# A decoder layer on one core: the divisions of probabilities shared out anew over three engines, moments asked two steps sooner, scale diagonals at a step's head

## The chip, the core and the metric

The kernel runs on 1 core of one Trainium2 chip. The metric is device time in microseconds (us), taken as the median of the runs shown; smaller is better. The engines of the core are named as in the profile: PE (TensorE matmuls and transposes), PEld (its weight loads), DVE (VectorE), ACT (ScalarE), POOL (GpSimd) and SP (SyncE, which here only issues DMAs).

## The reference

One pre-norm decoder layer over 8 batches of 256 rows of 1024 numbers, all in float32, with a self-attention, an attention to a context and a feed-forward block. Cut to what matters:

```python
# x: (8, 256, 1024), ctx: (8, 256, 1024)
def bitnet_linear(x, weight, scale):          # weights become signs, a scale per output column
    s = max(mean(abs(weight), axis=1), 1e-8)
    y = x @ sign(weight / s[:, None]).T
    return nan_to_num(y * (s * scale), nan=0, posinf=1e6, neginf=-1e6)

def self_attention(h):                        # 32 heads of 32, 8 key/value heads, each for 4 heads
    q, k, v = bitnet_linear(h, qw, qs), bitnet_linear(h, kw, ks), bitnet_linear(h, vw, vs)
    p = softmax(q @ k.T / sqrt(32))
    return bitnet_linear(p @ v, ow, os)

def cross_attention(h, ctx):                  # 16 heads of 64, low rank
    c_q, c_kv = h @ Wq_d, ctx @ Wkv_d
    p = softmax((c_q @ W_qk) @ c_kv.T / 8)    # per head
    return p @ (c_kv @ Wv_u)

def ffn(h):                                   # rank 256, inner 2752
    g, u = split((h @ U1) @ V1 + b1)
    return ((silu(g) * u) @ U2) @ V2 + b2

x = x + self_attention(layernorm(x))
x = x + cross_attention(layernorm(x), ctx)
out = x + ffn(layernorm(x))
```

The softmax of the self-attention is what the change is about: `p = exp(s - max)`, and then each row of `p` is divided by its sum.

## The kernel before

The work runs in three phases: 8 batches of self-attention, each in 8 steps c0 to c7 of 4 heads (class `Self`); 8 batches of cross-attention, each in 4 steps of 4 heads (class `Cross`); then the feed-forward block in 4 blocks of 512 rows. Batches are written b0 to b7 below, so that "b3 c6" is step 6 of the fourth self-attention batch.

The order of the instructions is written out by hand (a manual schedule): every engine executes its instructions in the order in which the Python code emits them, and an instruction that waits holds up everything behind it on its own engine.

One call of `step(cur, prev, parts)` emits, in this order:

- 16 score matmuls of the step's own 4 heads (L547) into four PSUM score banks;
- `due.early()` and `due.late()` for the step before the last: ACT copies its weighted sum `po` to `oh` (L601), DVE forms the rest `ol` (L605);
- for each head, the row maximum `nm` (L689, DVE), and `turned`: four transposes of the PREVIOUS step's `p` (L524, PE), whose result ACT copies to `pT` (L528). So the divisions of one step are needed at the head of the next;
- `parts` pieces of projection work from a queue of `Part`s: the layernorm transposes of the next batch (`ln_parts`: `xn` L155, transposes L163, `xh` L344, `xl` L345), its q, k and v projections (matmuls L399 and L466, ACT scaling L408, then `nan_to_num`: L351, L354, L357 on DVE and L352, L353 on POOL), and the output projection of the batch before (`o_parts`: matmuls L492, `y` L501, `nan_to_num`, the residual sum L506 on POOL). In b0 there are also the turning of weights into signs (`weight`: transposes L163, ACT sign L309, sums L298 to L303) and the `scale_part`s, which spread a column of scales over all partitions: POOL builds diagonals `dg` (L327), PE multiplies them by ones (L334), DVE copies (L335);
- between the parts, the 8 exponentials of the step with their sums (L708, ACT), paced by the estimated time of the parts, and, as soon as the sums of two heads are there, `over_sums`: the reciprocal (L560, DVE) and the divisions of these heads on DVE (L570, two instructions per head) or POOL (L563, one per head); after all parts, `over_sums_end` puts the divisions meant for ACT (L577, two per head);
- last the 16 weighted-sum matmuls of the previous step (L584).

Who divides is `self.by`, a letter for each of the four heads: D for DVE, P for POOL, A for ACT. Before, it is AAPP in b0; elsewhere DPAA in c1 and c2, DDAA in c0 and c4, and DDDA in the other steps.

A `Part` can have an `ahead` piece (the `xn` of a layernorm part, the `dg` of a scale part), which is emitted before the part itself: for the first two parts at the step's head, for a later one when the part before it starts. A part marked `soon` (the layernorm parts) has its `ahead` emitted at the step's head wherever it stands in the step.

The moments of a layernorm row tile (two `bn_stats` L138 and one `bn_aggr` L140 for each of two tiles, and two small POOL instructions at the end) are not parts: they wait in the list `idle` and are emitted one by one by `run_part`, one for each 1.4 us of estimated part time. `ln_moments` puts those of the next batch but one at the list's front; `leave` puts those of a finished residual at its end. `need` flushes the list when a layernorm needs them.

All parts, the transposes and the projections take their PSUM bank from `bank()`, which turns through three banks; a bank is free again when the engine that copies it out (ACT or DVE) has done so.

Of the kernel before, what the change touches and what calls it, by code (L numbers as in the profile page):

```python
# [35 lines left out]
def decoder_layer(  # L36
# [25 lines left out]
    B, S, E = x.shape  # L62
    NT = B * S // P
    TB = S // P
    EC = E // P
# [41 lines left out]
    def bank(shape, name):  # L107
        turn[0] += 1
        if turn[0] % 3 == 1:
            return psB.tile(shape, F32, tag="psB", name=name)  # L110
        return psA.tile(shape, F32, tag="psA", name=name)
# [13 lines left out]
    idle, credit = [], [0.0]  # L125
# [46 lines left out]
    def settle():  # L172
        now = list(ripe)
        ripe[:] = later
        later.clear()
        for f in now:
            f()
# [3 lines left out]
    class Part:  # L181
        def __init__(self, us, main, ahead=None, soon=False):
            self.us, self.main, self.todo, self.soon = us, main, ahead, soon
# [5 lines left out]

    queue = []  # L190

    def run_part(then=None):

        settle()
        if then is not None:
            then()
        p = queue.pop(0)
        p.ahead()
        if queue:
            queue[0].ahead()  # L200
        p.main()
        credit[0] += p.us
        while idle and credit[0] > 1.4:
            credit[0] -= 1.4
            idle.pop(0)()
        if not idle:
            credit[0] = 0.0
# [7 lines left out]
    o_sc = wt.tile([P, E], F32, tag="o_sc", name="o_sc")  # L215
# [55 lines left out]
    for i in range(len(room), len(where)):  # L271
        last = max(k for k in range(i) if where[k] == where[i])
# [40 lines left out]
    def weight_next(i):  # L313

        weight_turn(i)
        weight_sum(i)
        for k in after.get(i, []):
            weight_load(k)

    def scale_part(col0, n, dst):  # L320

        box = {}

        def ahead():
            box["dg"] = wk_.tile([P, n, P], F32, tag="xn", name="dg", bufs=2)
            for k in range(n):
                nc.gpsimd.tensor_scalar_mul(  # L327
                    box["dg"][:, k, :], ident, scol[:, col0 + k : col0 + k + 1]
                )

        def main():
            ps = bank([P, n, P], "ps_d")
            for k in range(n):
                nc.tensor.matmul(ps[:, k, :], ones, box["dg"][:, k, :], start=True, stop=True)  # L334
            nc.vector.tensor_copy(dst, ps.rearrange("p k c -> p (k c)"))  # L335

        return Part(0.3 * n, main, ahead)

    def weight(i):
        return Part(1.1, lambda: weight_next(i))  # L340
# [97 lines left out]
    def q_parts(st, c0):  # L438
        return proj_T(
            st, lambda i, e: qT_w[c0 + i][:, e, :], c0, lambda: st.qT[:, c0 : c0 + 2, :]  # L440
        )
# [89 lines left out]
    class Self:  # L531


        def __init__(self, st, c):
            self.st, self.c = st, c

            self.by = (
                "AAPP" if st.b == 0 else "DPAA" if c in (1, 2) else "DDAA" if c % 4 == 0 else "DDDA"
            )

        def scores(self):
            st, c = self.st, self.c
# [29 lines left out]
        def over_sums_end(self):  # L572
            for j in range(4):
                if self.by[j] == "A":
                    for t in range(TB):
                        p = self.p[j][:, t, :]
                        nc.scalar.activation(p, p, AF.Copy, scale=self.sm[:, t, j : j + 1])  # L577

        def weighted(self, pTs):
            self.po = pso.tile([P, S], F32, tag="pso", name="po")  # L580
# [98 lines left out]
    def step(cur, prev, parts, extra=None):  # L679

        s = cur.scores()
        nm = small.tile([P, 4, TB], F32, tag="nm", name="nm")
        cur.sm = small.tile([P, TB, 4], F32, tag="sm", name="sm")
        due = prev.prev if prev is not None else None
        if due is not None:
            due.early()
        pTs = []
        for j in range(4):
            nc.vector.tensor_reduce(nm[:, j, :], s[j], AX.X, ALU.max, negate=True)  # L689
            if prev is not None:  # L690
                pTs.append(turned(prev.p[j]))
        for p in queue[: min(parts, 2)]:
            p.ahead()
        soon = [p for p in queue[:parts] if p.soon][:2]
        if isinstance(due, Cross):
            for p in soon:
                p.ahead()
        if due is not None:
            due.late()
        for p in soon:  # L700
            p.ahead()
        cur.p, cur.prev = [], prev
        exps = []

        def exp(j, t):
            if t == 0:
                cur.p.append(wk_.tile([P, TB, S], F32, tag="p", name="p", bufs=4))
            nc.scalar.activation(  # L708
                cur.p[j][:, t, :], s[j][:, t, :], AF.Exp,
                bias=nm[:, j, t : t + 1], accum_out=cur.sm[:, t, j : j + 1],  # L710
            )

        exps = [(j, t) for j in range(4) for t in range(TB)]


        divided = isinstance(cur, Self)
        pe, sc = 0.0, 0.5 if divided else 1.0
        pairs = [0, 1]
        for k in range(parts):
            pe += queue[0].us  # L720
            while exps and sc < pe:
                exp(*exps.pop(0))
                sc += 0.49

            def then():
                while k and divided and pairs and len(exps) <= 4 - 4 * pairs[0]:
                    cur.over_sums(pairs.pop(0))

            run_part(then)
            if k == 0 and extra is not None:  # L730
                extra()
        for e in exps:
            exp(*e)
        for i in pairs:
            cur.over_sums(i)
        cur.over_sums_end()
        if not parts and extra is not None:
            extra()
        if prev is not None:
            prev.weighted(pTs)  # L740
            prev.prev = None
        return cur
# [365 lines left out]
        nc.sync.dma_start(of[fb.i * BT + j], fb.x[j])  # L1108


    sts, xts = [], []
    for b in range(B):
        for l in (sts, xts):
            st = State()
            st.b = b
            l.append(st)

    def mixed(a, b):
        out = []
        for i in range(max(len(a), len(b))):  # L1120
            out += a[i : i + 1] + b[i : i + 1]
        return out
# [4 lines left out]
    def self_plan(b):  # L1127
        st = sts[b]
        if b == 0:
            nxt = sts[1]  # L1130
            v0 = v_parts(st)
            ln, k, v = ln_parts(nxt, 1), k_parts(nxt), v_parts(nxt)
            return [
                [weight(4), weight(5), v0[0], scale_part(10, 2, v_sc)]
                + [weight(6), v0[1], weight(7)],
                mixed(q_parts(st, 2) + q_parts(st, 4), [weight(8), weight(9), weight(10)]),
                mixed(q_parts(st, 6), [weight(11), weight(12)]),
                ln[:2] + [weight(13)] + ln[2:],
                mixed(k, [weight(14), weight(15)]),
                mixed(v, [weight(16), weight(17)]),  # L1140
                mixed(q_parts(nxt, 0), [weight(18), scale_part(12, 4, o_sc[:, 0:512])])
                + [weight(19)],
                mixed(q_parts(nxt, 2), [scale_part(16, 4, o_sc[:, 512:1024])]),
            ]
        o = o_all(sts[b - 1])
        if b + 1 < B:
            nxt = sts[b + 1]
            ln = ln_parts(nxt, b + 1)
            return [
                q_parts(st, 4) + q_parts(st, 6),  # L1150
                mixed(o[0], ln[:2]),
                mixed(o[1], ln[2:]),
                k_parts(nxt),
                o[2] + v_parts(nxt),
                o[3],
                q_parts(nxt, 0),
                q_parts(nxt, 2),
            ]
        x0 = xts[0]
        ln = lnx_parts(x0)  # L1160
        return [
            q_parts(st, 4) + q_parts(st, 6),
            o[0],
            o[1],
            mixed(o[2], ln[:2]),
            mixed(o[3], ln[2:]),
            ctx_parts(x0, (dve, act)) + ckv_part(x0),
            cq_part(x0) + ckvT_part(x0),
            cqk_parts(x0, (dve, act)),
        ]  # L1170
# [16 lines left out]
    def self_extra(b, c):  # L1187
        if b == 0 and c == 1:
            return lambda: ln_moments(sts[1], 1)
        if b + 2 < B and c == EC - 1:  # L1190
            return lambda: ln_moments(sts[b + 2], b + 2)

    def cross_extra(b, c):
# [39 lines left out]
    with tc.manual_schedule(  # L1233
# [8 lines left out]
        st = sts[0]  # L1242
# [41 lines left out]
        prev = None  # L1284
        for kind, sts_, plan, loads, extra, n in (
# [3 lines left out]
            for b in range(B):  # L1289
# [3 lines left out]
                for c in range(n):  # L1293
                    loads(b, c)
                    prev = step(kind(sts_[b], c), prev, len(ps_[c]), extra(b, c))


        pairs = [(fb, f) for fb in fbs for f in range(NF)]
# [76 lines left out]
```

## Time and profile before

| what | value |
|---|---|
| median of the runs | 1572.12 us (1571.53 to 1572.9) |
| profiled execution, its own time | 1571.7 us |
| its span from first to last instruction | 1569.9 us |
| mean granted PE clock | 0.992 |
| busy: PE, DVE, ACT, POOL | 96%, 62%, 52%, 25% of the span |
| self-attention phase, and in it b0 | 25.5 to 653.9 us; 25.5 to 133.8 us |
| one whole batch (b2) | 74.5 us |
| cross phase and feed-forward after it | 653.9 us to the end |

The profile is of one execution; its rows give the start in us from the span's beginning, the busy time, the engine, the line of the kernel and the tiles that an instruction writes and reads. "[0.81 <-ACT pT L528]" behind a row says that the engine was idle for 0.81 us ahead of it and that ACT's write of `pT` ended this wait. PEclk is the clock granted to PE as a share of full speed. A step's borders are taken at its first score matmul (L547).

### The profile page before, as it was taken

How to read it: one execution, taken by the hardware profiler on the slowest of the kernel's cores; microseconds unless marked ns; L12 is line 12 of the kernel's file. 1: busy time of each engine (PE TensorE's matmuls, PEld its weight loads, DVE VectorE, ACT ScalarE, POOL GpSimd, SP SyncE). 2: the span in 40 equal slices, each digit the busy share in tenths (PEclk: the TensorE clock that was granted, in tenths of full speed). 3: DMA queues.
4: the chain of work that ended last, by engine and by line, in shares of the span. 5: the costliest groups of instructions: out<-in, count | busy, mean ns of one | idle time of the engine just before them, and what ended most of it. 6: DMA issues, size and time to landing. Idle time of an engine off the chain costs nothing.

```text
span 1569.9 us, 25667 instructions
## 1 busy us (share of the span) xinstructions
PE 1513.1 (96%) x9494; PEld 1015.9 (65%) x9494; DVE 973.0 (62%) x1880; ACT 811.4 (52%) x2482; POOL 390.5 (25%) x474
## 2 busy tenths in 40 slices
PE   6889999999999999899999999999999999999998
PEld 5777787787878787677877777544444444444443
DVE  6777999999899989766676666333233223323322
ACT  3787888888888888745556666311111110111110
POOL 2435444444444434123221111100010002001102
PEclk9999999999999999999999999999999999999999
DMA  9420010101010132112254312120001002000001
GB/s 232 91 55 15 28 57 27 68 21 62 28 55 28 52 105 95 60 39 97 82 201 145 130 47 90 59 69 0 0 41 67 0 0 107 0 1 27 27 0 53
DMA packets 65611, 92.77 MB, mean 59 GB/s; under 512 B 40218, under 2 KB 46160, under 8 KB 65360
## 3 DMA queue, kind: packets, MB, share of 16 engines
q1 hardware_dynamic: 60880, 74.37, 15.3%
q0 software_dynamic: 4608, 16.78, 2.7%
q8 instruction: 75, 1.23, 0.3%
q14 instruction: 48, 0.39, 0.1%
HBM read 65.44 MB, written 25.17 MB: 58 GB/s over the span
## 4 chain that ended last, share of the span: by engine, by line
PE 77%; DVE 14%; ACT 6%; DMA 1%; issue 1%; POOL 0%; SPq 0%; POOLq 0%; DVEq 0%; ACTq 0%
PE ps_h L1034 19%; PE ps_z L1078 9%; PE ps_pt L524 8%; PE ps_o L492 5%; PE ps_q L399 5%; PE s L622 4%; PE po L645 4%; PE ps_p L1008 4%; DVE nm L689 4%; PE ps_o L1097 3%; ACT p L708 3%; PE s L547 2%; PE po L584 2%; PE ps_o L662 2%; PE ps_qk L863 2%; DVE p L570 2%
## 5 line engine op out<-in xcount | busy, mean ns | idle before, releaser
L708 ACT ACTIVATE p<-s,nm 128x256 f32<-128x256 f32 x768 | 357.7, 516 | 2.2 <-DVE nm L689 2.2
L528 ACT COPY pT<-ps_pt 128x512 f32<-128x512 f32 x384 | 198.4, 598 | 147.9 <-PE ps_pt L524 147.2
L1046 ACT ACTIVATE sg<-ps_h,b_col 128x512 f32<-128x512 f32 (+1 forms) x88 | 59.6, 678 | 413.5 <-PE ps_h L1034 413.5
L689 DVE TENSOR_REDUCE nm<-s 128x2 f32<-128x512 f32 x384 | 237.4, 679 | 10.0 <-PE s L622 6.8
L1047 DVE SCALAR_TENSOR_TENSOR sg<-ps_h,b_col,sg 128x512 f32<-128x512 f32 (+1 forms) x88 | 65.0, 739 | 274.4 <-ACT sg L1046 274.4
L524 PE MATMUL ps_pt<-ident,p 128*128 128x128 f32 x1536 | 196.4, 278 | 10.2 <-ACT pT L528 6.6
L524 PEld LDWEIGHTS ps_pt<-ident,p 128*128 128x128 f32 x1536 | 164.4, 141 | 51.8 <-issue 21.9
L708 ACT ACTIVATION_READ_ACCUMULATOR p<-s,nm 128x1 f32 x768 | 189.8, 247 | 0.0
L1107 POOL TENSOR_TENSOR x2t<-x2t,y 128x512 f32<-128x512 f32 x32 | 40.5, 1267 | 482.5 <-DVE y L1105 482.5
L1078 PE MATMUL ps_z<-ac,u_sb 128*128 128x512 f32 x336 | 157.7, 593 | 0.0
L399 PE MATMUL ps_q<-xh,qT_w 128*128 128x256 f32 x496 | 121.9, 287 | 1.1 <-ACT qT_w L309 1.1
L399 PE MATMUL ps_q<-xl,qT_w 128*128 128x256 f32 x496 | 118.9, 281 | 0.0
L352 POOL TENSOR_SCALAR tmp<-y 128x512 f32<-128x512 f32 x78 | 60.8, 780 | 216.5 <-DVE y L501 127.4
L1078 PEld LDWEIGHTS ps_z<-ac,u_sb 128*128 128x128 f32 x336 | 61.9, 190 | 68.8 <-issue 68.8
L492 PE MATMUL ps_o<-oT_w,oh 128*128 128x512 f32 x256 | 105.8, 413 | 0.0
L570 DVE TENSOR_SCALAR p<-p,sm 128x256 f32<-128x256 f32 x252 | 99.0, 448 | 9.6 <-DVE sm L560 1.4
L677 POOL TENSOR_TENSOR x1t<-x1t,y 128x256 f32<-128x256 f32 x64 | 47.6, 764 | 224.7 <-DVE y L670 224.7
L492 PE MATMUL ps_o<-oT_w,ol 128*128 128x512 f32 x256 | 100.9, 394 | 0.0
L577 ACT ACTIVATE p<-p,sm 128x256 f32<-128x256 f32 x200 | 87.8, 512 | 17.8 <-DVE sm L560 17.6
L399 PEld LDWEIGHTS ps_q<-xh,qT_w 128*128 128x128 f32 x496 | 93.3, 188 | 2.8 <-ACT qT_w L309 1.4
L399 PEld LDWEIGHTS ps_q<-xl,qT_w 128*128 128x128 f32 x496 | 93.4, 188 | 0.0
L1034 PE MATMUL ps_h<-pT,w_ffn 128*128 128x512 f32 (+1 forms) x184 | 88.7, 577 | 0.0
(159 smaller groups left out, 2736.4 us busy)
## 6 DMA issues: line engine op xcount, KB each, us to landing
xs<-in_x_dram SPq DMA_DIRECT2D x32, 512.0 KB, 4.1
x<-xs POOLq DMA_DIRECT2D x16, 512.0 KB, 3.0
x1t<-x SPq DMA_DIRECT2D x16, 512.0 KB, 6.0
c<-in_ctx_dram SPq DMA_DIRECT2D x16, 512.0 KB, 3.9
x<-x1t POOLq DMA_DIRECT2D x16, 512.0 KB, 3.8
x2t<-x SPq DMA_DIRECT2D x16, 512.0 KB, 5.8
out_dram<-x2t SPq DMA_DIRECT2D x16, 512.0 KB, 2.6
w<-in_L_attn_q_weight_dram SPq DMA_DIRECT2D x32, 128.0 KB, 5.7
```

Of the source, the lines that this page charges most:

```text
L399: nc.tensor.matmul(ps[:, i, :], w(i, e), x_[:, e, :], start=(e == 0 and x_ is st.xh), stop=(e == EC - 1 and x_ is st.xl),)
L492: nc.tensor.matmul(ps, o_[c // 4][:, c % 4, t * P : (t + 1) * P], oT_w[:, c, h * 512 : (h + 1) * 512], start=(c == 0 and o_ is st.oh), sto ...
L524: nc.tensor.transpose(ps[:, k, t * P : (t + 1) * P], p[:, t, k * P : (k + 1) * P], ident)
L528: nc.scalar.copy(pT, ps)
L570: nc.vector.tensor_scalar_mul(p, p, self.sm[:, t, j : j + 1])
L577: nc.scalar.activation(p, p, AF.Copy, scale=self.sm[:, t, j : j + 1])
L622: nc.tensor.matmul(s[2 * i + j][:, t, :], st.cqk[p0 : p0 + XD, 2 * c + i, t * P : (t + 1) * P], st.ckv[p0 : p0 + XD, :], start=True, stop= ...
L689: nc.vector.tensor_reduce(nm[:, j, :], s[j], AX.X, ALU.max, negate=True)
L708: nc.scalar.activation(cur.p[j][:, t, :], s[j][:, t, :], AF.Exp, bias=nm[:, j, t : t + 1], accum_out=cur.sm[:, t, j : j + 1],)
L1034: nc.tensor.matmul(ps[h * n : h * n + n], v1_of(r, i, f, n), fb.pT[:, r, h * w_ : (h + 1) * w_], start=(r == 0), stop=(r == RC - 1),)
L1047: nc.vector.scalar_tensor_tensor(sg[:m], hs[0][:m], bg, sg[:m], ALU.add, ALU.mult)
L1078: nc.tensor.matmul(fb.zs[r], fw.u2[f // 4][:n, f % 4, r * P : (r + 1) * P], ac[:n], start=(k == 0), stop=(k == NF - 1 and COPIES < 2),)
```

## The change

1. `self.by` is now read from a table `BY` of a string per step. In b0: DDDD, PPPD, PPPD, PPPP, PPPD, PPPD, DDDD, PPPD. In b1 to b6 only c1 and c2 change, from DPAA to PPAA. In b7, c1 and c2 become DDDA, c3 and c4 PPAA. In all, ACT loses 34 divisions (L577), POOL gains 17 (L563, one for a whole head), and DVE has as many as before: 26 more in b0, 24 fewer in b1 to b6, 2 fewer in b7.
2. The moments of the next batch but one are asked at c5 instead of c7.
3. The two scale parts of `o_sc` (b0 c6 and c7) are marked `soon`, so that their `dg` diagonals are built at the step's head.
4. `over_sums_end` is called before a part of over 1.0 us as soon as both pairs of heads are done, and not again later (the letters are blanked). It moves instructions only in c0 of b1 to b7, where ACT's four divisions now stand ahead of the last q scaling (L408).
5. In the last part of a step, `run_part` emits no moments (`last`).
6. In the very first step the exponentials are paced 2.5 us later (`sc` 3.0).

The orders of PE and of SP are the same in both kernels; those of DVE, ACT and POOL change.

```diff
-    def run_part(then=None):
+    def run_part(then=None, last=False):
...
-        while idle and credit[0] > 1.4:
+        while not last and idle and credit[0] > 1.4:
             credit[0] -= 1.4
             idle.pop(0)()
...
-    def scale_part(col0, n, dst):
+    def scale_part(col0, n, dst, soon=False):
...
-        return Part(0.3 * n, main, ahead)
+        return Part(0.3 * n, main, ahead, soon)
...
-            self.by = (
-                "AAPP" if st.b == 0 else "DPAA" if c in (1, 2) else "DDAA" if c % 4 == 0 else "DDDA"
-            )
+            self.by = st.by[c]
...
+            self.by = "    "          # at the end of over_sums_end
...
-        pe, sc = 0.0, 0.5 if divided else 1.0
+        pe, sc = 0.0, (0.5 if prev is not None else 3.0) if divided else 1.0
...
+            if divided and not pairs and queue[0].us > 1.0:
+                cur.over_sums_end()
...
-            run_part(then)
+            run_part(then, k == parts - 1)
...
+    BY = {
+        0: ["DDDD", "PPPD", "PPPD", "PPPP", "PPPD", "PPPD", "DDDD", "PPPD"],
+        1: ["DDAA", "PPAA", "PPAA", "DDDA", "DDAA", "DDDA", "DDDA", "DDDA"],
+        B - 1: ["DDAA", "DDDA", "DDDA", "PPAA", "PPAA", "DDDA", "DDDA", "DDDA"],
+    }
...
-                mixed(q_parts(nxt, 0), [weight(18), scale_part(12, 4, o_sc[:, 0:512])])
+                mixed(q_parts(nxt, 0), [weight(18), scale_part(12, 4, o_sc[:, 0:512], True)])
                 + [weight(19)],
-                mixed(q_parts(nxt, 2), [scale_part(16, 4, o_sc[:, 512:1024])]),
+                mixed(q_parts(nxt, 2), [scale_part(16, 4, o_sc[:, 512:1024], True)]),
...
-        if b + 2 < B and c == EC - 1:
+        if b + 2 < B and c == 5:
             return lambda: ln_moments(sts[b + 2], b + 2)
```

More of the change, by code (lines that the diff above doesn't have):

```diff
@@ L1115, in decoder_layer @@
             st.b = b
+            st.by = BY.get(b, BY[1])
             l.append(st)
```

## The prediction

> **What bounds the kernel now.** I read the page's busy line and chain first, then the list of what PE waits for, then windows of single steps.
>
> ```profile
> span 1569.9 us, 25667 instructions
> PE 1513.1 (96%) x9494; PEld 1015.9 (65%) x9494; DVE 973.0 (62%) x1880; ACT 811.4 (52%) x2482; POOL 390.5 (25%) x474
> PE 77%; DVE 14%; ACT 6%; DMA 1%; issue 1%; POOL 0%; SPq 0%; POOLq 0%; DVEq 0%; ACTq 0%
> ```
>
> PE is the bound, and the change leaves its instructions and their order alone. So only PE's lost time can be won, and new lost time is the only way to lose. I measured it per step: the step's length less its PE instructions at their undisturbed pitch (0.119 us for a 128x256 projection matmul, 0.232 for a 128x512 one, 0.109 for a transpose). An undisturbed step shows 0.60 by this measure. The steps above that: b0 c0 9.6, c1 3.0, c2 3.3, c3 6.9, c4 2.2, c5 1.6, c6 6.6 (c7 none); in b2 to b6 c1 1.60, c2 0.87, c3 1.75 (b1 only c3); b7 c4 2.1, c5 3.3, c7 2.95. In b1 to b6, c0 and c4 to c7 stand at the floor. The waits in PE's list that the change touches:
>
> ```profile
> PE ps_pt L524 <- ACT pT L528: 6.6, 8, 1.1
> PE ps_d L334 <- POOL dg L327: 6.4, 2, 4.0
> PE ps_t L163 <- DVE xn L155: 4.4, 6, 0.8
> ```
>
> (us in all, times, longest.) They sum to 17.4, most of what can be won.
>
> **The scale diagonals at the head of b0 c6.** Timeline:
>
> ```profile
> 116.58 2.22 POOL L563 TENSOR_TENSOR p<-p,sm 128x512 f32<-128x512 f32 x2 [0.49 <-DVE sm L560]
> 118.79 2.56 POOL L327 TENSOR_SCALAR dg<-ident,scol 128x128 f32<-128x128 f32 x4
> 119.63 2.57 PE L334 MATMUL ps_d<-dg,ones 128*128 128x128 f32 x8 [4.03 <-POOL dg L327]
> ```
>
> The four `dg` stand behind two divisions on POOL, and PE waits 4.03 us; its clock is at half from 117.51 to 124.34. With `soon` they stand at the step's head, where POOL is free, and the two POOL divisions of c6 are gone (DDDD). The wait goes (4.0), and so does most of the half clock (c6 loses 6.6, floor 0.6, other transposes 0.7). I take −4.9. No DMA is issued by the moved pieces, and SP's queue is untouched.
>
> What is late next is c7. In c6 DVE now does eight divisions (DDDD, 8 × 0.35 = 2.8 us) and the first moments, where it did neither; behind them in its queue are `nm` of c7 and L335, which come some 2.4 us late: the exponentials and one transpose group waits 1.35, and the second `ps_d`, whose `dg` needs the column scale of the last weight (L298, 1.20, then L300 to L303), waits 1.35 where before it was covered by the stall of c6. c7: +2.9.
>
> At this place a rule speaks. Row: the clock halved at 117.51 in a 4.03 gap, but also at 32.18 after one gap of 1.23 in a stretch of sparse transposes. The Trainium skill, "TensorE: Matmul & The Clock Gate", Part 1, table of the two states, lets the clock fall after an idle window of about 3.4 us. By the rule the new gaps (1.35) in c7 are harmless: sum as it stands. By the row the clock could fall again there: 32 matmuls at 0.21 (their pitch in 32.18 to 33.65) instead of 0.119, +2.9. c7 is dense apart from its two gaps, so I take the rule and leave 2.9 in the range.
>
> **The rest of b0.** c0: the `v_sc` diagonals wait 2.4 behind two POOL divisions (AAPP to DDDD): −1.5 (between −1 and −2.5, by the clock, which is at half there). The later exponentials (`sc`) come in ACT's idle time: 0 while ACT is idle 2 us at a time (34 to 36 us), some +0.5 if not. c1: no divisions on ACT ahead of the `pT` copies, −0.65. c3: −0.5. c2, c4, c5: 0, their losses are in the weights' turning. b0 in all: −1.5 −0.65 −0.5 −4.9 +2.9 = −4.65. In b0, 32 ACT divisions of 0.51 (16 us) go to DVE and POOL, where they cost nothing as long as these are idle (69% and 44% busy in b0).
>
> **The moments two steps earlier, b1 to b5.** What they delay now, at c1 of the next batch:
>
> ```profile
> 299.17 0.63 PE L163 MATMUL ps_t<-ident,xn 128*128 128x128 f32 x4 [0.78 <-DVE xn L155]
> ```
>
> Two bn_stats and an aggregate (0.68 + 0.21 + 0.64, from 294.71) stand ahead of the row maxima and `xn` of c1. They belong to the queue's tail, which the moments of the next batch but one push back; these now come at c6 and c7, so the tail is done within c0. c1: −0.95 × 5 = −4.75. c2, same reason: −0.25 × 5 = −1.25. The loads that the moments read were issued by 309.10, well before c6 (340.43).
>
> The price is in c6 and c7, where DVE is full. Windows (us, then busy of PE, PEld, DVE, ACT, POOL):
>
> ```profile
> 340.43:348.31 7.88, 7.88 (x84) 6.69 (x81) 7.37 (x16) 7.17 (x25) 3.39 (x3) 1.00 0.01 3
> 348.31:356.20 7.89, 7.89 (x84) 6.71 (x80) 6.89 (x19) 7.61 (x26) 2.60 (x3) 1.00 0.18 70
> ```
>
> DVE is busy 7.37 of 7.88; two bn_stats and an aggregate add 1.45. They come ahead of L357, and after it this chain stands:
>
> ```profile
> 345.47 0.73 DVE L357 COPY_PREDICATED z<-fin,y 128x512 f32<-128x512 uint8 x1
> 346.29 1.29 POOL L506 TENSOR_TENSOR xs<-xs,z 128x512 f32<-128x512 f32 x1 [2.32 <-DVE sm L560]
> 346.76 1.75 DVE L570 TENSOR_SCALAR p<-p,sm 128x256 f32<-128x256 f32 x4 [0.47 <-DVE sm L560]
> 348.43 0.17 DVE L560 RECIPROCAL sm<-sm 128x4 f32<-128x4 f32 x1
> 348.63 0.91 ACT L577 ACTIVATE p<-p,sm 128x256 f32<-128x256 f32 x2
> 350.08 1.07 ACT L528 COPY pT<-ps_pt 128x512 f32<-128x512 f32 x2 [0.28 <-PE ps_pt L524]
> ```
>
> L357 1.45 late, so L506 1.45 late; the first division stalls until L506 ends (as here, 346.76 to about 347.7), now to 349.1; three more, the second reciprocal at 349.6, ACT's two divisions and the `oh` copy behind it, the first `pT` at 351.25 instead of 350.08. The banks turn by threes, so the fourth group of transposes comes at 351.9 instead of 350.7. [...]c7: +1.1 × 5 = +5.5, with +0.2 × 5 left over in c0. If the slack between 350.08 and PE's need is larger than I read it, 0; if it isn't recovered in c0, 4.4 a batch (c7 to c2).
>
> **The table in b1 to b6.** c1 and c2 from DPAA to PPAA. At c3's head:
>
> ```profile
> 309.57 2.41 DVE L570 TENSOR_SCALAR p<-p,sm 128x256 f32<-128x256 f32 x2
> 310.74 1.09 POOL L563 TENSOR_TENSOR p<-p,sm 128x512 f32<-128x512 f32 x1
> 313.30 1.09 PE L524 MATMUL ps_pt<-ident,p 128*128 128x128 f32 x8 [0.19 <-DVE y L501]
> 314.38 0.68 DVE L345 TENSOR_TENSOR xl<-ps_t,xh 128x512 fp32r<-128x512 f32 x1
> 315.20 1.06 PE L524 MATMUL ps_pt<-ident,p 128*128 128x128 f32 x8 [0.81 <-ACT pT L528]
> ```
>
> Two divisions on DVE take 2.41, for the first stalls behind POOL's L506 (309.49 to 310.78). Without them DVE comes sooner to L345 and the second reciprocal; but POOL's second division then runs to about 313.6, L351 stalls behind it, and `xl` frees its bank only 0.55 late instead of 1.15. c3: −0.6 × 6 = −3.6 (0 to −1.1 each).
>
> **b7 and the feed-forward's head.** c3 gets two more DVE divisions from c2, ahead of `nm`: +0.35. c3 and c4 have PPAA for DDDA and DDAA, so `cT` and `xT` copies free their banks sooner: c4 −1.5 of 2.1, c5 −1.35 of 3.3. c7: one more bn_stats ahead of the divisions, +0.6. Together −1.9. Of the head of the feed-forward (L524 to L662, 0.64 lost to `ol` L655 behind four bn_stats) −0.6: those statistics move into feed-forward steps, in which DVE idles over 2.5 us of every 5.15. `last` costs 0 by this; `over_sums_end` in c0 puts 4 × 0.5 on ACT ahead of L408, in steps that stand at the floor with four parts of PE work behind them: 0, at most +0.3 each.
>
> **Sum.** b0 −4.65; b1 to b6 −4.75 −1.25 −3.6 +5.5 +1.0 = −3.1; b7 −1.9; head −0.6: −10.25. The profiled execution took 1571.7 (1.8 beside its span); 1561.5. The median lies 0.4 above it: 1562.
>
> **Rivals.** (A) The moments' cost in c6 and c7 doesn't show (slack, or the scheduler of idle pieces spreads them): −10.25 −6.5 = −16.7, 1555. For it: c6 and c7 lose nothing now. Against: DVE 7.37 of 7.88.
> (B) Slower: the late second reciprocal isn't recovered in c0 but is handed from step to step (each step's divisions are needed at the next one's head): 4.4 × 5 = 22 instead of 6.5, −16.7 + 22 = +5.3, 1577. It decides from 16.7 / 5 = 3.3 us a batch on. Against it: c0 has 11.69 us and four parts.
> (C) No change: b0 gains nothing, since c7 pays back what c6 wins (half clock again +2.9, weight chain later), and c3 gains nothing: −10.25 + 4.65 + 3.6 = −2.0, 1570; with c7 a little dearer, 1575. For it: b0 is limited by the turning of weights on ACT and DVE, to which DVE's 26 extra divisions add 9 us.
>
> **How the numbers follow.** Chances: the forecast 0.54, A 0.20, B 0.16, C 0.10. About 3.1 us (0.2%) is what a measurement of this kernel can tell. Forecast and A are faster, with a tenth of C: 0.75; most of C and the mild end of B the same: 0.09; the rest slower, 0.16. The range: the forecast's own is 1556 to 1568 (c3 0 to −1.1, c7 half to double, b0 −2 to −10); downward it takes in A to 1553, upward C to 1574, leaving out B's bulk and A's far end, 2 in 10.
>
> **What would show it.** After: no wait of PE for `dg` in c6 and a clock of 1.00 there; c7 of b0 11 to 12 us instead of 8.78; c1 of b2 to b6 at about 8.7 instead of 9.66; c3 at about 8.4 instead of 9.03; c7 of b1 to b5 about 9.0 instead of 7.89, with PE waiting for `pT`. Wrong if c7 stays at 7.9 (A), if c0 to c2 grow by a microsecond each (B), or if b0's length stays at 108.3 (C).

## The result and the profile after

The changed kernel takes 1563.26 us (median, 1562.34 to 1563.68) against 1571.88 for the kernel before: a ratio of 0.9943, with a 95% interval of 0.9926 to 0.9961. That is 8.6 us less; the forecast was 1562, that is 10.25 less. The head of the page after:

```profile
span 1561.4 us, 25705 instructions
PE 1511.6 (97%) x9494; PEld 1013.4 (65%) x9494; DVE 965.2 (62%) x1880; ACT 799.3 (51%) x2448; POOL 406.6 (26%) x491
PE 76%; DVE 13%; ACT 7%; issue 2%; POOL 1%; SPq 1%; DMA 0%; POOLq 0%; DVEq 0%; ACTq 0%
```

PE is still the bound, with the same 9494 instructions. In the list of what PE waits for, these lines have changed (some line numbers have moved by up to two: L570 is now L568, L563 is L561, L577 is L575, L560 is L558):

- `pT` has gone from 6.6 to 2.5: c3 of b1 to b6 no longer waits for it, c7 of b1 to b5 now does, 0.4 each.
- `dg` has gone from 6.4 to 4.0: the wait of 4.03 in b0 c6 is gone and 0.49 has come in c7, but the one in b0 c0 has grown from 2.39 to 3.54.
- `xn` has the same sum, 4.5 after 4.4, but not the same waits: the five of about 0.8 in c1 of b2 to b6 are gone, and 3.6 has come in b0 c3 and 0.9 in b7 c3.
- Two lines have come up: an `xl` copy (c3 of b1 to b5, 0.4 each) and `p` itself, of which 1.7 is in b7 c7 (1.2 before) and 0.3 in b3 c7.

```profile
PE ps_t L163 <- DVE xn L155: 4.5, 4, 1.6
PE ps_d L334 <- POOL dg L327: 4.0, 2, 3.5
PE ps_pt L524 <- ACT pT L528: 2.5, 6, 0.5
PE ps_pt L524 <- DVE xl L345: 2.1, 5, 0.4
PE ps_pt L524 <- DVE p L568: 2.0, 3, 1.5
```

The lengths of the steps, from first score matmul to first score matmul, in both traces, against the forecast's terms (us):

| where | before | after | difference in all | forecast |
|---|---|---|---|---|
| head of the kernel | 25.50 | 25.83 | +0.3 | 0 |
| b0 c0 | 18.61 | 15.94 | −2.7 | −1.5 |
| b0 c1 | 16.66 | 15.94 | −0.7 | −0.65 |
| b0 c2 to c5 | 47.00 | 47.30 | +0.3 | −0.5 |
| b0 c6 | 17.29 | 12.74 | −4.6 | −4.9 |
| b0 c7 | 8.78 | 11.52 | +2.7 | +2.9 |
| c1 of b2 to b6 | 9.67 | 8.69 | −4.9 | −4.75 |
| c2 of b2 to b6 | 8.93 | 8.72 | −1.0 | −1.25 |
| c3 of b1 to b6 | 9.03 | 8.33 | −4.2 | −3.6 |
| c7 of b1 to b5 | 7.89 | 9.37 | +7.4 | +5.5 |
| c0 of b1 to b6 | 11.69 | 11.72 | +0.2 | +1.0 |
| b7 | 74.19 | 73.45 | −0.7 | −1.9 |
| feed-forward's head | | | −0.6 | −0.6 |
| sum | | | −8.5 | −10.25 |

(The rows of b1 to b6 give the mean of a step.) All else is unchanged within 0.3. The spans differ by the same 8.5. In b0 PE's clock was at half for 23.9 us before and for 6.8 us after, so that b0's lengths hold a gain in clock besides the waits.

b0 c6 in windows of its step and the next (us, then busy of PE, PEld, DVE, ACT, POOL, and PEclk), after:

```profile
105.01:117.75 12.74, 11.05 (x109) 9.42 (x105) 12.25 (x28) 8.98 (x27) 6.51 (x13) 1.00 0.01 3
117.75:129.27 11.52, 10.07 (x93) 7.89 (x89) 9.73 (x19) 7.11 (x23) 8.15 (x13) 1.00 0.01 1
```

The clock is at 1.00 throughout. The diagonals start 5.3 us into the step (11.0 before), and the wait of 4.03 for them is gone, with 0.78 for an earlier bank in its place:

```profile
110.33 2.39 POOL L327 TENSOR_SCALAR dg<-ident,scol 128x128 f32<-128x128 f32 x4
113.69 1.13 PE L334 MATMUL ps_d<-dg,ones 128*128 128x128 f32 x8 [0.78 <-ACT oT_w L309]
```

And the new loss, at b3 c6 and c7, in the timeline of DVE, POOL, ACT and PE after:

```profile
341.00 0.21 DVE L140 BATCH_NORM_AGGREGATE mv<-st 128x2 f32<-128x12 f32 x1
341.12 0.70 DVE L357 COPY_PREDICATED z<-fin,y 128x512 f32<-128x512 uint8 x1
341.91 1.27 POOL L506 TENSOR_TENSOR xs<-xs,z 128x512 f32<-128x512 f32 x1 [3.72 <-DVE sm L558]
341.99 2.56 DVE L568 TENSOR_SCALAR p<-p,sm 128x256 f32<-128x256 f32 x4
343.26 0.61 POOL L352 TENSOR_SCALAR tmp<-y 128x512 f32<-128x512 f32 x1
344.08 1.89 PE L524 MATMUL ps_pt<-ident,p 128*128 128x128 f32 x11 [0.29 <-DVE p L568]
344.47 0.17 DVE L558 RECIPROCAL sm<-sm 128x4 f32<-128x4 f32 x1
344.67 0.91 ACT L575 ACTIVATE p<-p,sm 128x256 f32<-128x256 f32 x2 [1.96 <-DVE sm L558]
346.37 0.66 PE L524 MATMUL ps_pt<-ident,p 128*128 128x128 f32 x4 [0.41 <-ACT pT L528]
```

The order is that of the forecast: the moments end at 341.2, L357 follows 1.6 later in its step than before, L506 with it, and the four divisions stretch from 341.99 to 344.55 (2.56 us; 1.75 before). The second reciprocal comes 2.0 late and ACT idles 1.96 for it.

### The profile page after: what moved, and what is told of

Same layout as the page of the kernel before. It is cut to its first block, busy times and chain, and to the rows that moved or that the text cites. A ratio compares the mean times of both kernels' runs of the same rounds, so it can differ in the third digit from the quotient of the medians.

```text
span 1561.4 us, 25705 instructions
## 1 busy us (share of the span) xinstructions
PE 1511.6 (97%) x9494; PEld 1013.4 (65%) x9494; DVE 965.2 (62%) x1880; ACT 799.3 (51%) x2448; POOL 406.6 (26%) x491
## 3 DMA queue, kind: packets, MB, share of 16 engines
q8 instruction: 75, 1.23, 0.3%
## 4 chain that ended last, share of the span: by engine, by line
PE 76%; DVE 13%; ACT 7%; issue 2%; POOL 1%; SPq 1%; DMA 0%; POOLq 0%; DVEq 0%; ACTq 0%
PE ps_h L1036 19%; PE ps_z L1080 9%; PE ps_pt L524 7%; PE ps_q L399 7%; ACT p L707 4%; PE s L621 4%; PE po L644 4%; PE ps_p L1010 4%; PE ps_o L1099 3%; PE ps_o L492 3%; DVE nm L688 3%; PE s L545 2%; PE po L583 2%; PE ps_o L661 2%; PE ps_qk L865 2%; PE ps_q L850 2%
## 5 line engine op out<-in xcount | busy, mean ns | idle before, releaser
L352 POOL TENSOR_SCALAR tmp<-y 128x512 f32<-128x512 f32 x78 | 57.6, 738 | 182.8 <-DVE y L501 121.1
L568 DVE TENSOR_SCALAR p<-p,sm 128x256 f32<-128x256 f32 x252 | 94.1, 430 | 8.0
L1036 PE MATMUL ps_h<-late,w_ffn 128*128 128x512 f32 (+1 forms) x184 | 88.7, 577 | 0.0
```

The costliest lines, as they stand in the source:

```text
L568: nc.vector.tensor_scalar_mul(p, p, self.sm[:, t, j : j + 1])
L1036: nc.tensor.matmul(ps[h * n : h * n + n], v1_of(r, i, f, n), fb.pT[:, r, h * w_ : (h + 1) * w_], start=(r == 0), stop=(r == RC - 1),)
```

## The experiments

All but the last three take the changed kernel and undo or move one thing or a few. The differences below are those of step lengths in the profile of one execution each, against the changed kernel. Where the code of a step is the same, its length still differs between traces: b0 c0 by up to 1.3, b0 c3 by 0.7 and b0 c4 by 0.5, for a reason that stands under "The clock" below; elsewhere by less than 0.1 in most steps, with a single step now and then 0.3 to 0.9 off.

**The moments' place, b1 to b5.** Moments asked at c7 again:

```diff
-        if b + 2 < B and c == 5:
+        if b + 2 < B and c == EC - 1:
```

> The changed kernel with the moments of the next batch but one asked at c7 again; all else as changed. My account (the moments made both c1's gain and c7's loss): c7 of b1 to b5 back from 9.4 to 7.9 (-7.4 in all), c1 of b2 to b6 back from 8.70 to 9.66 (+4.9), c2 +0.2 each (+1.0), the feed-forward's head +0.6, b7 c7 -0.6: -1.5, about 1562. Rival (c1's gain came from the shares PPAA in c1 and c2, the moments only cost): c1 stays at 8.70, about 1556.

Measured: 1559.59 us (ratio to the kernel before 0.992, 0.9903 to 0.9937), 3.7 below the changed kernel. c7 is back at 7.9 as expected, and b0 c6 and c7 are 1.4 and 1.6 shorter, which had not been expected. c1 stayed at 8.70, as the rival had it; but c2 grew by 1.2 to 9.9, and neither expectation had that. The DVE timeline of this kernel in b3 c1 shows why: the bn_stats now stand behind `xn`, not ahead of it.

```profile
288.67 0.53 DVE L155 TENSOR_SCALAR xn<-xs,mv,rs 128x512 f32<-128x512 f32 x1
289.92 0.68 DVE L138 BATCH_NORM_STATS2 st<-xs 128x6 f32<-128x512 f32 x1
290.76 1.23 DVE L138 BATCH_NORM_STATS2 st<-xs 128x6 f32<-128x512 f32 x2
292.81 0.66 DVE L345 TENSOR_TENSOR xl<-ps_t,xh 128x512 fp32r<-128x512 f32 x1
```

`last` bars them from c0's last part, so they come after c1's first part. To part the two, `last` was taken away, without and with the moments at c7:

```diff
-            run_part(then, k == parts - 1)
+            run_part(then)
```

> The changed kernel with moments allowed in a step's last part again (no `last`); the moments still asked at c5. Then two bn_stats stand ahead of the row maxima of c7 in b1 to b5 and two ahead of L357 there fall away. If the moments' earlier place makes c1's gain by itself: c1 of b2 to b6 stays at 8.70. If `last` makes it: c1 back to 9.66 (+4.8 in all). c7: the row maxima 1.5 us late, 9.0 to 9.7 as now. The time 1563 by the first, 1568 by the second.

> The changed kernel with the moments asked at c7 again and without `last`: the moments stand as in the kernel before, only the shares and the diagonals are changed. If `last` alone took the bn_stats out of c1's way where the moments were undone alone (c1 8.70, c2 9.87 there): c1 of b2 to b6 9.66 and c2 8.7 to 8.9 here, c7 7.9, the time 1558 to 1559.5. If the shares PPAA made c1's gain: c1 8.70 and c2 about 8.7, the time 1554.

Without `last` but with the moments at c5: 1562.82 us (0.9939, 0.9923 to 0.9956), c1 of b2 to b6 still at 8.70, c7 at 9.3. With the moments at c7 too: 1559.33 us (0.9916, 0.9902 to 0.9931), c1 back at 9.6 to 9.67, c2 at 9.0, c7 at 7.88. So the earlier moments make c1's gain by themselves, and the shares PPAA have no part in it; `last` without them merely hands the loss on to c2. Set against the moments at c7 with `last`, the earlier ones win 5.9 in c2 but cost 7.4 in c7 and 3.0 in b0: as placed, they are a net loss of 3.7. Taking `last` away from the changed kernel also made b7 c7 0.59 shorter and the feed-forward's head 0.61 and x3 (the fourth cross batch) 0.21 longer: those terms of the forecast were `last`'s, and cancel.

**What makes c7 late.** The moments in c6 and c7 of b1 to b5 stay in their step but stand behind L357 of the second part (`full` is set there):

```diff
         settle()
+        if full[0] and last:
+            moments_now()
         if then is not None:
             then()
...
-        while not last and idle and credit[0] > 1.4:
-            credit[0] -= 1.4
-            idle.pop(0)()
+        if not last and not full[0]:
+            moments_now()
```

> The changed kernel with one thing moved: in c6 and c7 of b1 to b5 the moments stand behind L357 of the step's second part instead of ahead of it, so that POOL's residual sum L506 runs beside the bn_stats and not beside the divisions. If the chain through L357, L506 and the stalled division makes c7 late: the second reciprocal of c6 1.3 us sooner, c7 8.0 to 8.5 instead of 9.4, the time 1557 to 1559. Rival (DVE simply has 1.5 us too much to do in c6, whatever the order): c7 stays above 9.1, the time 1562 to 1563.

Measured: 1559.56 us (0.9921, 0.9907 to 0.9936), less 3.7. c7 is 7.9 in all five batches; c0 behind it is 12.39 instead of 11.7, because in c7 three bn_stats now come ahead of the divisions. b3 c6 in the timeline of DVE and POOL (this kernel's lines are 8 higher from L199 on: L365 is L357, L514 is L506, L576 is L568):

```profile
337.90 0.73 DVE L365 COPY_PREDICATED z<-fin,y 128x512 f32<-128x512 uint8 x1
338.52 1.27 DVE L138 BATCH_NORM_STATS2 st<-xs 128x6 f32<-128x512 f32 x2
338.71 1.30 POOL L514 TENSOR_TENSOR xs<-xs,z 128x512 f32<-128x512 f32 x1 [2.32 <-DVE z L365]
340.18 1.14 DVE L576 TENSOR_SCALAR p<-p,sm 128x256 f32<-128x256 f32 x4
341.24 0.17 DVE L566 RECIPROCAL sm<-sm 128x4 f32<-128x4 f32 x1
```

The work is the same, yet the four divisions take 1.14 us instead of 2.56, because POOL's sum now runs beside the bn_stats, which it doesn't slow (1.27, as when POOL was idle). The chain through L357 and L506 with the stalled divisions made c7 late, and not DVE's load.

**The table in b1 to b6.** DPAA in c1 and c2 again:

```diff
-        1: ["DDAA", "PPAA", "PPAA", "DDDA", "DDAA", "DDDA", "DDDA", "DDDA"],
+        1: ["DDAA", "DPAA", "DPAA", "DDDA", "DDAA", "DDDA", "DDDA", "DDDA"],
```

> The changed kernel with DPAA in c1 and c2 of b1 to b6 again; all else as changed. My account: c3 of b1 to b6 back from 8.0-8.4 to 9.03 (+4.2 in all), c1 and c2 unchanged within 0.1, the time about 1567.5. Rival (c3's gain came from the moments, which left DVE earlier): c3 stays at 8.4, about 1563.

Measured: 1566.77 us (0.9966, 0.9954 to 0.9978), 3.5 above the changed kernel. c3 is back at 9.02 to 9.04 in five of the six batches and at 8.61 in b4, +3.8 in all; c1 and c2 are as they were. In the changed kernel L351 at c3's head takes 1.04 instead of 0.43, stalled behind the second of two POOL divisions, as forecast, and `xl` comes 1.78 after the step's start instead of 2.42:

```profile
305.46 2.04 POOL L561 TENSOR_TENSOR p<-p,sm 128x512 f32<-128x512 f32 x2
306.75 1.04 DVE L351 TENSOR_SCALAR z<-y 128x512 f32<-128x512 f32 x1
308.46 0.67 DVE L345 TENSOR_TENSOR xl<-ps_t,xh 128x512 fp32r<-128x512 f32 x1
309.28 1.06 PE L524 MATMUL ps_pt<-ident,p 128*128 128x128 f32 x8 [0.43 <-DVE xl L345]
```

**The diagonals of b0 c6 and c7.** Not marked `soon`:

```diff
-    scale_part(12, 4, o_sc[:, 0:512], True)
+    scale_part(12, 4, o_sc[:, 0:512])
...
-    scale_part(16, 4, o_sc[:, 512:1024], True)
+    scale_part(16, 4, o_sc[:, 512:1024])
```

> The changed kernel with the two scale parts of o_sc not marked soon, so that the diagonals stand again right before the part ahead of theirs; all else as changed, DDDD in b0 c6 too. If the place of the diagonals made the gain: PE waits some 4 us for dg in c6 again, b0 c6 about 16 instead of 12.74, the time 1565 to 1567. Rival (the gain came from the two POOL divisions that DDDD takes off POOL in front of the diagonals): no wait above 1 us, b0 c6 within 1 us of 12.74, the time 1563 to 1564.

Measured: 1567.76 us (0.9971, 0.9961 to 0.9981), 4.5 above the changed kernel. c6 is 20.41, longer than in the kernel before, and c7 2.7 shorter, 8.83; the clock is at half for 10.2 us of c6. (0.9 of this trace is a stretch at half clock in b7 c7, where its code is that of the changed kernel.) The place of the diagonals makes the gain, although POOL has no division in c6 here: they now stand behind the small POOL instructions for the next weight's column scale (L301 to L303), which wait for a sum on DVE (L298) behind that step's moments and first four divisions.

```profile
116.55 0.23 POOL L301 TENSOR_SCALAR total<-total 128x1 f32<-128x1 f32 x1 [1.58 <-DVE sm L558]
117.29 3.33 POOL L327 TENSOR_SCALAR dg<-ident,scol 128x128 f32<-128x128 f32 x4
118.92 2.55 PE L334 MATMUL ps_d<-dg,ones 128*128 128x128 f32 x8 [6.46 <-POOL dg L327]
```

**The table in b0.** AAPP in all its steps:

```diff
-        0: ["DDDD", "PPPD", "PPPD", "PPPP", "PPPD", "PPPD", "DDDD", "PPPD"],
+        0: ["AAPP"] * 8,
```

> The changed kernel with AAPP in all steps of b0 again, diagonals still at the head. My account: c0 +2 (PE waits for the v_sc diagonals behind two POOL divisions), c1 +0.7, c3 +0.5, c6 no wait for dg above 1 us, c7 1 to 2.7 shorter because DVE has no divisions in c6: the time 1562 to 1565. Rival (the shares DDDD and PPPD keep c6 clean, too): c6 above 15, the time 1567 or more.

Measured: 1562.69 us (0.994, 0.9925 to 0.9955), no difference that can be told from the changed kernel. c0 16.3 and c1 15.9 keep their gains, c6 is 11.6, and c7 is 12.4, longer still, without one DVE division in c6. (c3 and c4 are shorter by 0.6 and 0.4, but so they are in four traces that have the changed kernel's table there: that is the clock.) So neither c0's gain nor c7's loss came from the shares alone. Two more runs asked where c0's came from; the second also put `over_sums_end` back behind the parts:

```diff
-        pe, sc = 0.0, (0.5 if prev is not None else 3.0) if divided else 1.0
+        pe, sc = 0.0, 0.5 if divided else 1.0
...
-            if divided and not pairs and queue[0].us > 1.0:
-                cur.over_sums_end()
```

> The changed kernel with the exponentials of the very first step paced as before (sc 0.5); DDDD in b0 c0 stays. If the shares DDDD took the divisions out of the v_sc diagonals' way: c0 stays at 15.5 to 16.5, the time 1563. If only the later exponentials did: c0 back to 18, the time 1565.5.

> The changed kernel with AAPP in all of b0, the first exponentials paced as before, and over_sums_end only after all parts. POOL's two divisions of c0 stand ahead of the v_sc diagonals again, and ACT's four of each step behind the parts. If either the shares or the pacing is enough for c0 (AAPP alone left it at 16.3): c0 about 18.5; c1 about 16.6 if the early over_sums_end made c1's gain there: the time 1565 to 1566. If c0's and c1's gains lie elsewhere: 1562.5 to 1563.5.

Only the pacing undone: 1564.01 us (0.9954, 0.9938 to 0.9971), which can't be told from the changed kernel; in its one trace c0 is 17.96, which is +2.0, nearer to its rival. AAPP, pacing and early end undone: 1568.72 us (0.9975, 0.9964 to 0.9985), c0 19.1 and c1 16.68. In this last kernel POOL's two divisions stand ahead of the diagonals again:

```profile
34.28 2.04 POOL L561 TENSOR_TENSOR p<-p,sm 128x512 f32<-128x512 f32 x2 [0.18 <-DVE sm L558]
36.31 1.23 POOL L327 TENSOR_SCALAR dg<-ident,scol 128x128 f32<-128x128 f32 x2
```

With AAPP and the later exponentials they come at 40.42, behind the diagonals (33.77), and PE idles 3.71 us in c0 instead of 6.25; with DDDD and the exponentials as before it idles 4.24. So either edit clears POOL for the diagonals. But in the changed kernel, which has both, POOL divides nothing in c0, and the later exponentials must act in another way. PE there even waits longer for the diagonals than in the kernel with only the pacing undone. First the changed kernel, then that one:

```profile
34.93 1.09 PE L334 MATMUL ps_d<-dg,ones 128*128 128x128 f32 x4 [3.54 <-POOL dg L327]
```

```profile
35.34 1.40 PE L334 MATMUL ps_d<-dg,ones 128*128 128x128 f32 x4 [1.18 <-POOL dg L327]
```

What differs is what comes before, and the clock. With the exponentials as before, ACT's copies of turned weights (L309) stand between them, and PE waits 1.14 and 1.23 us for these; with the later ones the four copies are done from 27.60 to 29.67 without a break, and PE reaches the diagonals 5.6 us into the step instead of 8.6. The clock is at half for 10.2 us of c0 in the one kernel and for 3.4 in the other. The traces with the later exponentials have c0 at 15.5 to 16.8, those without at 18.0 to 19.1. How much of this is the pacing and how much where the fall of the clock happens to come is not shown: the nine traces with the changed kernel's code in c0 have 3.4 us at half in four and 6.8 in five. c1's 0.7 is made by the early `over_sums_end` where heads are divided on ACT: with AAPP, c1 is 15.9 with it and 16.7 without.

**A better mix.** The moments behind L357 in c6 of b1 to b5 only, b0's moments at c7 as before, b7's c1 and c2 as before:

```diff
+                    full[0] = kind is Self and 1 <= b <= 5 and c == 6
...
-        if b + 2 < B and c == 5:
+        if b + 2 < B and c == (5 if b else EC - 1):
...
-        B - 1: ["DDAA", "DDDA", "DDDA", "PPAA", "PPAA", "DDDA", "DDDA", "DDDA"],
+        B - 1: ["DDAA", "DPAA", "DPAA", "PPAA", "PPAA", "DDDA", "DDDA", "DDDA"],
```

> The changed kernel with three things: the moments behind L357 in c6 of b1 to b5 only (c7 as changed), b0's moments asked at c7 as before, and DPAA in c1 and c2 of b7 as before. If the parts add up: c7 of b1 to b5 7.9 (-7.3) with c0 at 11.7, b0 c6 11.3 and c7 9.9 (-3.0), b7 c3 8.7 (-1.0): about 1552. If b0's moments at c7 make b1 late instead, or b7 c4 grows with DPAA: 1554 to 1556.

Measured: 1552.7 us (0.9875, 0.986 to 0.9889), 10.6 below the changed kernel: faster than both. c7 of four of the five batches of b1 to b5 is 7.9 (b3's 8.6, which is 7.9 in the two versions below), c0 stays at 11.7 to 11.8, b0 c6 and c7 are 11.3 and 9.9, b7 c3 8.7; b7 c4 grew by 0.4. The parts add up. Two versions of it, with AAPP in b0 c6 and in all of b0:

> The mixed kernel of before (moments behind L357 in c6 of b1 to b5, b0's moments at c7, DPAA in c1 and c2 of b7) with AAPP instead of DDDD in b0 c6. If c7 of b0 is late because of DVE's eight divisions in c6: c7 about 9.0 instead of 9.9, the time 1551.8. If the two divisions on POOL take their place ahead of the column scale's chain there: c7 10 to 12, 1552.7 to 1554.5.

> The mixed kernel with AAPP in all steps of b0. If b0's table is worth nothing (AAPP alone moved the changed kernel by -0.6): within 1 us of 1552.7. If its steps c3 and c4 gain as they did there (-1.0) and c6 and c7 don't lose: 1551.7; if c7 loses 2.5: 1555.

Measured: 1553.27 us (0.9877, 0.9862 to 0.9892), b0 c7 10.5 instead of 9.9; and 1552.92 us (0.9873, 0.9858 to 0.9887). Both are the same as the mix within what can be told, and b0's table is worth nothing here either. Taking DVE's divisions out of c6 doesn't make c7 sooner; but AAPP puts two divisions on POOL, ahead of the small instructions for the column scale, so that what DVE's divisions cost by themselves stays open.

## Why the prediction was right

**The sum.** It lay within 1.5 us of the measured median, and seven of its thirteen terms within a half. The others were off by 0.6 to 1.9, in both directions, so that the nearness of the sum is in part luck. That the change left PE's order alone, so that each step's lost time could be followed through the engine queues that feed it, is what made it work. Three of the largest mechanisms were shown: the diagonals at the step's head (without `soon`, c6 +7.7), the moments ahead of `xn` in c1 (the pair of runs without `last`) and the shares in c1 and c2 as the source of c3's gain.

**c7 of b1 to b5** was mis-sized: +7.4, not +5.5. The mechanism was right (moving L357 ahead of the moments took all of it away in c7), but the step "then three more" divisions at their own pitch failed: the second one stalled too, 0.77 us, behind POOL's L352, which follows L506 directly once L506 is late. The second reciprocal came 2.0 late, not 1.2. The step "+0.2 left over in c0" was too dear: at most 0.09 a batch.

**b0** came out right in its sum, −4.9 against −4.65, but in two of its steps the cause was not the one named, or not it alone, and part of the rest is luck of the clock. For c0 it let the wait for the `v_sc` diagonals go and put the later exponentials at "0". The wait grew, from 2.39 to 3.54; what c0 won is that PE reached the diagonals sooner and stood at half clock for 3.4 us instead of 10.2, and there the later exponentials have a part. For c7 it put the delay to DVE's eight divisions besides the moments, with two waits of 1.35 (which make 2.7, not 2.9). Without those divisions c7 was no shorter (12.4, though two of them then stood on POOL), and without the moments c6 and c7 together were 3.0 shorter. It was right that the stall of c6 had covered work of c7: with all of DVE's divisions and moments in c6, but with the stall back (no `soon`), c7 is 8.83 again, as before. What keeps the rest of c7's loss without the moments (9.9 against 8.8) stays open.

**b7** won 0.75, not 1.9. The failing step is "two more DVE divisions from c2": DPAA to DDDA is four more (two heads, two instructions each), and c3's `xn` came 1.2 later in its step, so c3 lost 1.03 and not 0.35; c5 won 0.94 and not 1.35. With DPAA back c3 was 8.70. The last 0.6 of b7 c7 and of the feed-forward's head are effects of `last`, which the forecast had costed at 0 and put to the moments; they cancel.

**The clock.** The forecast took the Trainium skill's rule ("TensorE: Matmul & The Clock Gate", Part 1, the table of the two states: a fall after an idle window of about 3.4 us) over the row of 32.18. In the changed kernel the clock stayed at 1.00 in c6 and c7 of b0, so that nothing of the 2.9 came due.

But the traces follow neither the page's idle window nor the longest gap. Every stretch at half clock in b0 lasts 3.41 us, or two or three times that, and in each trace the stretches start on one grid of 3.41 us: in the kernel before at 32.18, 79.97 and 117.51, the last two 14 and 25 times 3.413 after the first. The falls follow how busy PE was in the window of the grid just before. Two windows of the kernel before, and two of the changed kernel, each followed by half clock (PE's busy time is the second number behind the window; PEclk is the third from the end):

```profile
28.77:32.18 3.41, 1.71 (x13) 1.47 (x13) 3.16 (x6) 3.41 (x11) 0.59 (x3) 1.00 1.03 260
114.10:117.51 3.41, 1.50 (x13) 1.30 (x11) 1.81 (x4) 2.85 (x10) 1.52 (x4) 1.00 0.00 0
```

```profile
33.12:36.53 3.41, 1.41 (x8) 0.98 (x8) 1.83 (x7) 0.04 (x1) 2.18 (x5) 1.00 0.65 106
77.49:80.91 3.42, 1.45 (x16) 1.02 (x20) 3.02 (x5) 2.27 (x8) 2.90 (x5) 1.00 0.02 5
```

And the same code as in that last row, in the kernel with the moments at c7, whose grid lies otherwise; the clock didn't fall:

```profile
76.14:79.55 3.41, 2.03 (x15) 1.61 (x16) 3.21 (x7) 3.16 (x12) 0.74 (x1) 1.00 0.00 1
79.55:82.96 3.41, 1.85 (x23) 0.91 (x21) 2.55 (x5) 2.25 (x8) 2.17 (x5) 1.00 0.02 5
```

Over all fourteen traces, from 13 to 1540 us: all 22 windows at full clock in which PE was busy 46% or less were followed by half clock, of those from 47 to 51% 4 of 15, and of the 6185 above that none. The page's table asks for an idle window; here a window need not be idle, and the measurement decides. The fall at 32.18, with no gap above 1.23, is such a window (50%); the gap of 3.54 in the changed kernel ended before the clock fell. In c6 and c7 of that kernel no window had less than 71%. Since the grid can lie anywhere against the kernel's work, the same code can lose a stretch in one execution and not in another: b0 c3 and c4 together take 24.1 us with one and 23.1 without. That is the spread of b0's steps between traces.

**The rivals.** A (the cost in c6 and c7 hidden) and B (handed on to c0, c1, c2) both fell on the step lengths: c7 lost 1.48 a batch, c0 took 0.03. C fell with b0's 4.9.

## What to carry to other kernels

An engine that is "full" is not the same as an engine that makes others late: here 1.45 us of extra VectorE work cost 1.5 us a batch ahead of an instruction that starts a GpSimd sum, and behind it nothing in 14 of the 15 such steps of the mixed kernels. When work is moved into a busy step, look for the first instruction behind it that starts another engine, and put the extra work after that. And a pacing constant that moves exponentials moves everything behind them on their engine and everything that depends on their sums, down to another queue's order; cost it like an edit of those queues.

## What the runs showed of the hardware

VectorE's in-place division (128x256, 0.35 us alone) stalls here until the GpSimd instruction beside it ends: 1.33 us beside a sum of 1.27, and 0.77 beside a one-input TENSOR_SCALAR of 0.61. The bn_stats beside a sum of 1.30 took 1.27 for two, the same as alone. So the one instruction is held and the other isn't, and a short one-input GpSimd operation holds it as well; between them lies c7's loss. It isn't so beside everything: in b0 c0 of the changed kernel, where the four divisions had begun before L327, none took more than 0.38, and the first L327 took 0.94 instead of 0.60.

```profile
341.99 1.33 DVE L568 TENSOR_SCALAR p<-p,sm 128x256 f32<-128x256 f32 x1
343.25 0.77 DVE L568 TENSOR_SCALAR p<-p,sm 128x256 f32<-128x256 f32 x1
```
